# Seven slots for half tiles in each routing in place of eight

## The chip, the cores and the metric

The kernel runs on one core of a Trainium2 chip. The metric is the device time of one execution in microseconds (us). The engines of the core are TensorE (PE, matmuls; PEld is its loading of weights), VectorE (DVE), ScalarE (ACT) and GpSimd (POOL); SyncE (SP) issues most DMA transfers.

## The reference

The kernel computes two layers of a network on 4096 tokens (64 sequences of 64) of width 256, all in float32. The first layer (a scan over the condition, linear attention, a quantised feed-forward net) isn't touched by the change. The second layer has a recurrent net, a selective scan (Mamba), and then two mixtures of experts, one after the other, in each of which every token goes to 2 of 8 experts:

```python
# first mixture: routed experts with one hidden layer of 256, beside two shared experts
s = jax.nn.sigmoid(router_in @ W_router.T)
_, topk_idx = jax.lax.top_k(s + router_bias, 2)
...
for e in range(8):
    h = jax.nn.gelu(x_flat @ r_w1[e].T, approximate=False)
    routed_out = routed_out + h @ r_w2[e].T * gates_full[:, e:e + 1]
out = (shared_out + routed_out) / 4
# second mixture: gated experts with a hidden layer of 704, on the output of the first
topk_scores, topk_idx = jax.lax.top_k(xt @ Wg.T, 2)
y = W3[e] @ (silu(W1[e] @ t) * (W2[e] @ t))       # for the two experts e of token t
out = sum of topk_score * y over the two
```

## The kernel before, in words

**Routing.** A class `Routing` collects, for each expert, the rows of the tokens that chose it. There are three: moe0 and moe1 for the two halves of the tokens in the first mixture (4 chunks of 512 tokens, so 4096 rows for the experts each), and ffn1 for all tokens in the second (8 chunks, 8192 rows). `choose` finds the two experts of each token and the place of its row, `send` scatters the rows (260 numbers: the token's 256, two weights, the token's number and the rank of its first expert) into regions of device memory, one region to an expert, by indirect DMA on POOL (L1357).

**Tiles.** An expert's rows are worked off in whole tiles of 256 rows (`TR`) and half tiles of 128 (`HR`). How many rows an expert gets is known only on the chip; how many tiles run is fixed when the kernel is built. So each routing has slots: `ntl` for whole tiles (16 in moe0 and moe1, 32 in ffn1) and `NHT` for half tiles (8, one for each expert). `Routing.tiles` (L1463) writes a table, made of the counts by a chain of small VectorE instructions, with an expert and a first row for each slot. An expert's remainder of 1 to 128 rows takes a half tile, a remainder above 128 a whole one, and whole tiles for which no slot is left become two halves each. A slot that nobody needs points to filler rows and to expert 0, and is run all the same. The helper `listed` (L1384) fills the table for the whole and for the half slots, `ends` (L1433) makes running sums, `counts` (L1420) gets the counts with one matmul (L1426).

For ffn1, a first table of 8 whole tiles (`EARLY`, L1443) is made when half of the tokens are routed; the remaining 24 whole and all half slots come from `tiles` at the end.

**Running the tiles.** `Experts.run` takes the sections in order; among n whole tiles the halves are spread evenly: after whole tile i come the halves from i * halves // n to (i + 1) * halves // n. For each tile SP reads the expert's number and row from the table (L1637), loads the expert's weights w (L1557; 512 KB in the first mixture, 2176 KB in the second) and the rows gx (L1365), some tiles ahead: 4 in the first mixture (`Gelu`), 2 in the second (`Swiglu`). PE transposes the rows (L1571), VectorE copies them (gxT, L1573) and works out where results go and by what they are weighted (L1576 to L1586). Then:

- `Gelu`: 8 records of up products (L1665), one activation on ACT (rh, L1667), the down products (acc, L1596), weighting on ACT (gy, L1598), scatter on POOL (L1372).
- `Swiglu`: 40 records of up products for the hidden columns in blocks of 128 (L1698) and 4 for the rest (L1706), an activation (gs, L1701) and a product on VectorE (gh, L1702) for each block, then the down products, weighting and scatter as above.

A half tile has the same number of up products with 128 columns in place of 256, half of the transposes and half of the down products. Each logical float32 matmul shows as two records.

**Order of the work.** `mixtures` (L1940) writes the order by hand. Generators are advanced beside the tiles: `tiles_on` steps the tile generator, which yields three times for a tile of the first mixture and nine times in the second, and for each step advances others by a fixed share. Beside moe0's tiles lie the last routing work of moe1 (`rest`) and the last shared experts (L1843, L1859); then the last tiles of moe0 and first of moe1 run alone, while moe1's table is made; beside the rest of moe1 lies the gate of the second mixture for the first four chunks (`gates`: SP loads the shared rows, L1879, and the routed rows, L1381; VectorE adds them, L1886; PE scores them, L1513). The 8 early tiles of ffn1 have the other four chunks beside them, and the last 24 whole and 8 half tiles run alone. The number of tiles in a routing, n + NHT, enters the counts in `tiles_on`. At the end all results are gathered, transposed and added (L2052).

Of the kernel before, what the change touches and what calls it, by code (L numbers as in the profile page):

```python
# [13 lines left out]
F32 = mybir.dt.float32  # L14
# [3 lines left out]
ALU = mybir.AluOpType  # L18
AX = mybir.AxisListType
PSUM = bass.MemoryType.PSUM  # L20

P = 128
# [1129 lines left out]
NE = 8  # L1152
TT = CH // P
TR = 256
HR = TR // 2
NHT = NE
EARLY = 8
assert EARLY * TR <= NT - NE * (TR - 1)

# [90 lines left out]
class Routing:  # L1250
# [10 lines left out]
    def __init__(self, g, pool, x, name, chunks, lots):  # L1261
# [6 lines left out]
        self.taken = None  # L1268
        self.y = g.tc.dram_tile((2 * NT + 2 * TR * (self.ntl + NHT), D), F32, name=f"{name}_y")
        tile = lambda shape, dt, n: pool.tile(shape, dt, name=f"{name}_{n}")  # L1270
# [192 lines left out]
    def tiles(self, pool):  # L1463


        nc = self.g.nc
        ntl = self.ntl - (EARLY if self.taken is not None else 0)
        out = self.tables(pool, ntl + NHT, "tiles")
        with self.g.tc.tile_pool(name=f"{self.name}_table", bufs=1) as work:
            n, first_t = self.counts(work)  # L1470
            col = lambda name: work.tile([P, NE], F32, name=name)

            nk = self.reg // TR
            unit = work.tile([P, NE, 2, nk], F32, name="unit")
            nc.gpsimd.iota(unit, [[0, NE], [HR, 2], [TR, nk]], base=0, channel_multiplier=0, allow_small_or_imprecise_dtypes=True)
            nc.vector.tensor_tensor(unit, n.unsqueeze(2).unsqueeze(3).to_broadcast([P, NE, 2, nk]), unit, ALU.is_gt)
            both = work.tile([P, NE, 2], F32, name="units")
            nc.vector.tensor_reduce(both, unit, AX.X, ALU.add)
            pairs, halves = both[:, :, 1], col("halves")
            nc.vector.tensor_sub(halves, both[:, :, 0], pairs)  # L1480
            if self.taken is not None:
                nc.vector.tensor_sub(pairs, pairs, self.taken)
                nc.vector.scalar_tensor_tensor(first_t, self.taken, float(TR), first_t, ALU.mult, ALU.add)
            begin, end = self.ends(work, pairs, "t")

            over, t = col("over"), col("over_b")
            nc.vector.tensor_scalar(over, end, -float(ntl), 0.0, ALU.add, ALU.max)
            nc.vector.tensor_scalar(t, begin, -float(ntl), 0.0, ALU.add, ALU.max)
            nc.vector.tensor_sub(over, over, t)
            first = col("first_h")  # L1490
            nc.vector.scalar_tensor_tensor(halves, over, 2.0, halves, ALU.mult, ALU.add)
            nc.vector.tensor_sub(first, pairs, over)
            nc.vector.scalar_tensor_tensor(first, first, float(TR), first_t, ALU.mult, ALU.add)
            begin_h, end_h = self.ends(work, halves, "h")
            self.listed(work, out, [(0, ntl, TR, begin, end, first_t), (ntl, NHT, HR, begin_h, end_h, first)])
        return out
# [35 lines left out]
class Experts:  # L1532
# [9 lines left out]
    def run(self, sections):  # L1542
# [71 lines left out]
        def more():  # L1614
            for v in islice(tiles, 1):
                load_rows(v)
                ahead.append(v)
# [322 lines left out]
def mixtures(g, mix, x, weights, out, last, work, close):  # L1940
# [9 lines left out]
    def tiles_on(tiles, n, *beside):  # L1950

        at = 0
        for mark in tiles:
            n -= mark is TILE
            if n == 0:
                break
            at += 1
            for pieces, many in beside:
                some(pieces, int(at * many) - int((at - 1) * many))

    with ExitStack() as ctx:
# [7 lines left out]
        tiles = Gelu(g, (q2, q3, qy, first), weights[0]).run(  # L1969
            [(moe0, lambda: mix.tables, n, NHT, None), (moe1, lambda: tables1[0], n, NHT, None)]  # L1970
        )
        n += NHT
        next(tiles)
        others, shared = mix.rest(last, work, q3), mix.shared(NCH - 1, last, work)
        for _ in range(5):
# [12 lines left out]
        def gates(chunks):  # L1988
# [10 lines left out]
            for c in chunks:  # L1999
# [12 lines left out]
                (routing, lambda: tables2[0], EARLY, 0, routing.sent),  # L2012
                (routing, lambda: tables2[1], ntl, NHT, None),
            ]
# [197 lines left out]
```

## Time and profile before

| | |
|---|---|
| median of 3 runs | 2756.78 us (2755.14 to 2759.66) |
| the profiled execution's own time | 2753.39 us |
| its span, first to last instruction | 2751.5 us |
| mean granted clock of PE | 0.936 |
| moe0 and moe1 tiles | about 1830 to 2133 us |
| early ffn1 tiles | about 2133 to 2265 us |
| last ffn1 tiles | about 2265 to 2707 us |
| gathering and output | to 2751.5 us |
| tables made on VectorE | moe0 up to 1741 us, moe1 1974 to 1980, ffn1 2251 to 2259 |

The profile's summary lists each engine's busy time and its share of the span. The 40 slices are 68.8 us each; a digit is the busy share in tenths, PEclk the clock that PE was granted. A line of the time line has the start in us, the duration, the engine, the source line, the operation, what is written and read, the tile's shape (partitions x elements) and the number of instructions merged; in brackets stands how long the engine was idle before, and who ended that. A line of the waits has the time in total, the number of times and the longest.

### The profile page before, as it was taken

The numbers are of one execution on the slowest core, as the hardware profiler recorded it, in microseconds if no ns is written. First come the engines' busy times: TensorE is split into PE (matmuls) and PEld (weight loads), VectorE is DVE, ScalarE is ACT, GpSimd is POOL, SyncE is SP. The second block draws the span as 40 slices with busy tenths as digits, with TensorE's granted clock in tenths as the row PEclk, the third lists the DMA queues.
The fourth block names the chain that finished last, engine by engine and source line by source line (L and its number), as shares of the span: only waits on it lengthen the run. The fifth ranks groups of instructions, "written<-read, shape, count | busy, mean of one in ns | idle before, by whom it ended". The sixth has DMA issues, their size and how long they took to land.

```text
span 2751.5 us, 34452 instructions
## 1 busy us (share of the span) xinstructions
PE 2310.7 (84%) x11996; PEld 1659.9 (60%) x11996; DVE 1752.4 (64%) x2952; ACT 1398.3 (51%) x2324; POOL 1371.9 (50%) x1194
## 2 busy tenths in 40 slices
PE   3979977997578888887888788788877989999995
PEld 3634435775345555554655555567655778888884
DVE  0467638982899898989889797952353443323333
ACT  0467627884676868685767666643232222222220
POOL 0013345530687878887889797935555331111110
PEclk9989988997769999999999999999998999999997
DMA  9999920002112222221222222226776765555555
GB/s 225 371 358 349 304 72 1 1 1 92 55 62 84 67 77 70 80 70 69 67 96 68 91 70 94 98 77 204 239 263 232 271 231 204 198 197 202 208 195 193
DMA packets 180502, 406.04 MB, mean 148 GB/s; under 512 B 24785, under 2 KB 84434, under 8 KB 174946
## 3 DMA queue, kind: packets, MB, share of 16 engines
q1 hardware_dynamic: 166882, 366.80, 39.0%
q0 software_dynamic: 13440, 36.98, 3.5%
q8 instruction: 96, 1.57, 0.2%
q14 instruction: 84, 0.69, 0.1%
HBM read 280.76 MB, written 144.98 MB: 155 GB/s over the span
## 4 chain that ended last, share of the span: by engine, by line
PE 46%; DVE 22%; ACT 11%; issue 9%; POOL 4%; DMA 2%; another core or an unknown queue 1%; SPq 0%; DVEq 0%; ACTq 0%; POOLq 0%
DVE hb L1108 13%; PE ps L1698 11%; PE acc L1596 9%; PE out L450 4%; DVE hb L1110 3%; PE ps L1665 2%; PE mq L1843 2%; PE yp L1123 2%; ACT dA L1063 2%; PE steps L820 1%; PE s L416 1%; POOL hb L1056 1%; PE acc L441 1%; PE ps L1706 1%; PE mp L919 1%
## 5 line engine op out<-in xcount | busy, mean ns | idle before, releaser
L1056 POOL TENSOR_TENSOR hb<-dx,Bn 128x1024 f32<-128x1024 f32 x256 | 604.9, 2376 | 178.2 <-PE yp L1123 130.8
L1108 DVE TENSOR_TENSOR_SCAN hb<-dA,hb 128x512 f32<-128x512 f32 x512 | 602.3, 1210 | 68.5 <-ACT dA L1063 67.7
L1063 ACT ACTIVATE dA<-delta,negA 128x504 f32<-128x504 f32 x512 | 345.0, 685 | 265.4 <-DVE hb L1108 258.6
L1123 PEld LDWEIGHTS yp<-ident,hb 128*128 128x128 f32 x2048 | 260.1, 149 | 158.4 <-issue 125.2
L1110 DVE TENSOR_TENSOR hb<-hb,cb 128x1024 f32<-128x1024 f32 x256 | 312.4, 1220 | 45.1 <-PE cb L1008 24.7
L1698 PE MATMUL ps<-gxT,w 128*128 128x256 f32 (+1 forms) x1600 | 324.7, 361 | 2.1 <-DVE gh L1702 0.8
L1698 PEld LDWEIGHTS ps<-gxT,w 128*128 128x128 f32 x1600 | 276.2, 190 | 48.4 <-issue 12.4
L1123 PE MATMUL yp<-ident,hb 128*128 128x128 f32 x2048 | 294.6, 286 | 0.0
L1843 PE MATMUL mq<-x,moe_s 128*128 128x256 f32 x896 | 238.2, 399 | 57.8 <-ACT sh L1847 25.8
L1372 POOL DMA_INDIRECT ffn_y<-gy,to x72 | 69.2, 961 | 430.8 <-ACT gy L1598 418.3
L1843 PEld LDWEIGHTS mq<-x,moe_s 128*128 128x128 f32 x896 | 164.3, 196 | 124.1 <-ACT sh L1847 42.9
L1702 DVE TENSOR_TENSOR gh<-gs,ps 128x256 f32<-128x256 f32 (+1 forms) x200 | 78.5, 394 | 211.6 <-ACT gs L1701 199.0
L1598 ACT ACTIVATE gy<-acc,wt 128x256 f32<-128x256 f32 x152 | 67.2, 474 | 250.6 <-PE acc L1596 218.8
L1701 ACT ACTIVATE gs<-ps 128x256 f32<-128x256 f32 (+1 forms) x200 | 72.5, 364 | 237.7 <-PE ps L1698 222.1
L1596 PE MATMUL acc<-w,gh 128*128 128x256 f32 (+1 forms) x864 | 188.2, 388 | 0.0
L1008 PE MATMUL cb<-parts,pick 80*128 80x512 bf16 x256 | 103.3, 404 | 89.2 <-DVE hb L1110 83.3
L1596 PEld LDWEIGHTS acc<-w,gh 128*128 128x128 f32 (+1 forms) x864 | 145.4, 189 | 30.2 <-issue 13.1
L432 POOL TENSOR_TENSOR E<-E,z 128x1024 f32<-128x1024 f32 x32 | 61.6, 1925 | 194.7 <-DVE z L431 117.2
L1372 POOL DMA_INDIRECT moe_y<-gy,to x80 | 77.9, 974 | 98.3 <-ACT gy L1598 73.8
L1596 PE MATMUL acc<-w,rh 128*128 128x256 f32 x320 | 86.3, 411 | 41.4 <-ACT rh L1667 26.4
L450 PE MATMUL out<-oT,hs 128*128 128x512 f32 x256 | 119.4, 611 | 1.5 <-ACT oT L443 1.5
L1859 PE MATMUL mq<-moe_s,sh 128*128 128x256 f32 x448 | 113.3, 386 | 6.6 <-ACT up L1850 2.9
(477 smaller groups left out, 4371.7 us busy)
## 6 DMA issues: line engine op xcount, KB each, us to landing
w<-ffn_w SPq DMA_DIRECT2D x40, 2176.0 KB
Bn<-B SPq DMA_DIRECT2D x128, 512.0 KB
moe_x<-fill SPq DMA_DIRECT2D x130, 260.0 KB
ffn_x<-fill SPq DMA_DIRECT2D x129, 260.0 KB
w<-moe_w SPq DMA_DIRECT2D x48, 512.0 KB
ffn_w<-in_ffn_W_dram SPq DMA_DIRECT2D x16, 640.0 KB
gx<-moe_x SPq DMA_DIRECT2D x32, 260.0 KB
gx<-ffn_x SPq DMA_DIRECT2D x32, 260.0 KB
```

Of the source, the lines that this page charges most:

```text
L450: nc.tensor.matmul(ps, M[:, o, ts(k, P)], v.o[:, o], start=(o == 0), stop=(o == H // 2 - 1))
L1008: nc.tensor.matmul(t, pick[:, n : n + 1].to_broadcast([rows, P]), v.parts, start=True, stop=True)
L1056: nc.gpsimd.tensor_mul(hb, vs[c].dx[p], Bn[:, n % NB, :].unsqueeze(1).to_broadcast([P, PI, CH]))
L1063: nc.scalar.activation(decays[s][i][:, :, 1:], seq(vs[c].delta[p][:, i, :])[:, :, 1:], AF.Exp, scale=A[:, p * PI + i, n : n + 1],)
L1108: ins = nc.vector.tensor_tensor_scan(h, dA[i].rearrange("p b l -> p (b l)"), h, 0.0, ALU.mult, ALU.add)
L1110: ins = nc.vector.tensor_tensor(hb, hb, cb.unsqueeze(1).to_broadcast([P, PI, CH]), ALU.mult)
L1123: nc.tensor.matmul(yp[i][:, t, :], hb[:, i, ts(t, P)], g.ident, start=(n == 0 and t == 0), stop=(n == S - 1 and t == CH // P - 1), is_tran ...
L1372: i = self.g.nc.gpsimd.indirect_dma_start(out=self.y, out_offset=bass.IndirectOffsetOnAxis(ap=to, axis=0), in_=y, in_offset=None)
L1596: nc.tensor.matmul(po[s], h, w, start=(i == 0), stop=(i == n - 1))
L1698: nc.tensor.matmul(ps[:, j, :], v.w12[:, k, ts(j * (full + 1) + i, P)], v.xT[:, k, :], start=(k == 0), stop=(k == KD - 1))
L1843: nc.tensor.matmul(ps[:, i % 2, :], w[:, k, ts(i, P)], xu[:, k, :], start=(k == 0), stop=(k == KD - 1))
L1859: nc.tensor.matmul(ps[:, t, :], h[:, i, ts(t, P)], self.s2[:, i, :], start=(i == 0), stop=(i == NS - 1))
```

## The change

The number of half slots becomes seven. The case in which all eight experts have a remainder of 1 to 128 rows is caught in the table: the minimum of the eight half counts (1 then, else 0) is added to the first expert's whole tiles and taken from its half tiles. The lines of the changed kernel behind the edit are four higher.

```diff
-NHT = NE
+NHT = NE - 1
...
             pairs, halves = both[:, :, 1], col("halves")
             nc.vector.tensor_sub(halves, both[:, :, 0], pairs)
+            all_half = work.tile([P, 1], F32, name="all_half")
+            nc.vector.tensor_reduce(all_half, halves, AX.X, ALU.min)
+            for n_e, sign in ((pairs, 1.0), (halves, -1.0)):
+                nc.vector.scalar_tensor_tensor(n_e[:, 0:1], all_half, sign, n_e[:, 0:1], ALU.mult, ALU.add)
             if self.taken is not None:
```

`NHT` stands in the number of half slots of all three routings, in the size of the table and of the results' buffer, and, through n, in the counts of `tiles_on` for moe0 and moe1. The halves are spread anew among the whole tiles: in ffn1 they stood after every third whole tile (3, 6, ... 24) and stand now after 4, 7, 11, 14, 18, 21 and 24; in moe0 and moe1 after every second one, and now after 3, 5, 7, 10, 12, 14 and 16.

## The prediction

> **What bounds the kernel now.** I read the summary first, then the 40 slices, then PE's time line in the stages that run expert tiles, because a slot is a tile that is run whether its rows are real or filler.
>
> ```profile
> PE 2310.7 (84%) x11996; PEld 1659.9 (60%) x11996; DVE 1752.4 (64%) x2952; ACT 1398.3 (51%) x2324; POOL 1371.9 (50%) x1194
> ...
> PE   3979977997578888887888788788877989999995
> ...
> PEclk9989988997769999999999999999998999999997
> DMA  9999920002112222221222222226776765555555
> ```
>
> No engine is full over the span, but from slice 33 on (2265 us) PE is at 9 tenths at full clock with DMA at 5: that is the last gated layer, with 24 whole and 8 half tiles. The table of stretches says it exactly: PE works in all of 435 us.
>
> ```profile
> 2265.00:2700.00 435.00, 435.00 (x2216) 370.73 (x2215) 132.09 (x473) 94.43 (x251) 54.86 (x58) 1.00 0.54 196
> ```
>
> The first number after the stretch is its length, the second PE's busy time. PE's time line shows one whole tile and the half tile behind it:
>
> ```profile
> 2310.67 8.90 PE L1698 MATMUL ps<-gxT,w 128*128 128x256 f32 x40
> 2319.40 1.03 PE L1706 MATMUL ps<-gxT,w 128*128 128x256 f32 x4
> 2320.27 0.38 PE L1571 MATMUL ps<-ident,gx 128*128 128x128 f32 x2
> 2320.49 5.12 PE L1596 MATMUL acc<-w,gh 128*128 128x256 f32 x24
> 2325.53 4.73 PE L1698 MATMUL ps<-gxT,w 128*128 128x128 f32 x40
> 2330.10 0.61 PE L1706 MATMUL ps<-gxT,w 128*128 128x128 f32 x4
> 2330.55 0.60 PE L1571 MATMUL ps<-ident,gx 128*128 128x128 f32 x4
> 2330.98 2.95 PE L1596 MATMUL acc<-w,gh 128*128 128x256 f32 x12
> 2333.86 2.43 PE L1698 MATMUL ps<-gxT,w 128*128 128x256 f32 x10
> ```
>
> No gap stands before any of them, so here a tile costs what its matmuls cost. The two mixtures (1830 to 2133 us) are another regime: a tile is short, and PE waits in each for ScalarE's activation (rh).
>
> ```profile
> 1987.32 1.99 PE L1596 MATMUL acc<-w,rh 128*128 128x256 f32 x8 [0.53 <-ACT rh L1667]
> 1989.14 1.05 PE L1665 MATMUL ps<-gxT,w 128*128 128x128 f32 x8
> 1990.04 0.60 PE L1571 MATMUL ps<-ident,gx 128*128 128x128 f32 x4
> 1990.73 1.13 PE L1596 MATMUL acc<-w,rh 128*128 128x256 f32 x4
> ...
> 1994.34 1.99 PE L1596 MATMUL acc<-w,rh 128*128 128x256 f32 x8 [0.31 <-ACT rh L1667]
> ...
> 1998.81 1.99 PE L1596 MATMUL acc<-w,rh 128*128 128x256 f32 x8 [0.53 <-ACT rh L1667]
> ```
>
> **What the change removes.** Three half tiles: one in each mixture's routing, one in the last layer. How many tiles run is fixed when the kernel is built, not by the data. The compiled order of instructions says the same: in moe0 and moe1 seven halves stand among 16 whole tiles, in the last layer seven among 24, and the last tile is a half as before.
>
> *Last layer.* From the first half (2325.53) to the next (2378.89 in the same view) is one group of three whole tiles and a half, 53.36 us; the chain of waits has all seven such distances equal. A whole tile between whole tiles takes 15.08 us (2280.50 to 2295.58). The group without its half would take 3 x 15.08 = 45.24, so the half is worth **8.12 us** (8.33 of its own, less 0.22 for the two transposes that its predecessor spares). Every half runs the same instructions, so which slot goes doesn't matter. Its weights (2176 KB) and rows go too; DMA stands at 0.54 of its time there, and PE waits for none of it. I take 8.12 with no play.
>
> By the Trainium skill ("TensorE: Matmul & The Clock Gate", Back-to-back issue gap) a stream of pairs of weight load and matmul sustains about 81 ns each at 128 columns. The row shows (2330.10 - 2325.53) / 40 = 114 ns; by the page the 44 matmuls of 128 columns would take 3.6 us in place of 5.0, and the gain would be an estimated 6.7 us. The row decides.
>
> *The mixtures.* In the uncrowded part, the group of two whole tiles and a half takes 1998.81 - 1987.32 = 11.49 us, and one whole tile behind another 1998.81 - 1994.34 = 4.47. So a half is worth 11.49 - 2 x 4.47 = **2.55 us**. Its PE work alone is near that: from 1989.14 to 1990.04 for the up product, 0.97 for the down product, 0.2 for two transposes, 2.1 in all. Most of the half tiles lie beside other work (the shared experts in moe0, the gate of the last layer in moe1). That work is dealt out by steps of the tile generator, three to a tile, so it stays beside the same number of tiles; with fewer halves among them one more whole tile lies beside it, and the uncrowded end loses one whole tile for it. If that other work, or the transfers, set the pace there, the whole tile is taken in free and the end loses up to 4.47; if what sets the pace cares for neither, nothing is gained. So 0 to 4.47 each, and I take 2.55, the only spacing that the trace shows: 5.10 for two.
>
> **What it adds.** Three small VectorE instructions in each of the three tables: a minimum over eight numbers and two updates of one number. No row has them; the nearest are the neighbours in the same table, here before the last layer:
>
> ```profile
> 2252.28 0.17 DVE L1480 TENSOR_TENSOR halves<-units 128x8 f32<-128x8 f32 x1
> 2252.47 0.17 DVE L1482 TENSOR_TENSOR units<-units,ffn_taken 128x8 f32<-128x8 f32 x1
> 2252.68 0.17 DVE L1439 TENSOR_TENSOR_SCAN endt<-onet,units 128x8 f32<-128x8 f32 x1
> ```
>
> Dependent ones start 0.2 us apart, independent ones 0.08. The minimum and the first update depend on what stands ahead, the second update doesn't: 2 x 0.2 + 0.08 = 0.48; the half-tile lists become 56 wide in place of 64, some 0.08 us less over eleven instructions. So **0.4 us** a table. Nothing hides it in two places. In the last layer's table VectorE works without a pause from 2251.2 to 2259.4, and the products gh (L1702) are queued behind it: PE loses 0.46 + 0.83 + 2.78 us to it today, and each further instruction is added. In moe1's table the copy gxT (L1573) is queued behind, and PE waits 1.56 us for it; SP waits 7.5 us for the table, which four tiles loaded ahead cover. moe0's table lies in the scan stage, where the scans (L1108) are queued behind it. So 0 to 0.6 a table, 0.4 taken, 1.2 in all.
>
> **Moved.** In the compiled order SP's loads of routed and shared rows (L1381, L1879) stand one tile load earlier or later among the loads of w and gx; the number of these row loads is the same, and POOL's scatters become one fewer per half. I cost this at nothing on average; its risk is the last rival.
>
> **Sum.** -8.12 - 5.10 + 1.2 = **-12.0 us**. The profiled execution took 2753.39 (span 2751.5 and 1.9 around it), so it would take 2741.4. It lies 3.4 us below the median of the three runs, 2756.78; against that the change gives **2744.8**. With the bounds: -8.12 - 8.94 + 0 = -17.1 (2739.7), and -8.12 - 0 + 1.8 = -6.3 (2750.5).
>
> **Rivals.** *The mixtures give nothing*: a chain of loads and scatters sets their pace. For it: between 2060 and 2108 us PE is busy only 29.8 of 48 us. Against it: from 1951 to 2013 it is busy 55 of 62, and the spacing of halves there is that of PE and rh. Then only the last layer is gained: -8.12 + 1.2 = -6.9, 2749.9.
>
> *A stall more or less.* Five times ScalarE's rh stands with no releaser that the profile knows:
>
> ```profile
> ACT rh L1667 <- remote: 30.0, 5, 9.2
> ```
>
> That is 30.0 us in all and 9.2 at the longest, at 1942 us, where PE, ScalarE and VectorE all stand while DMA is at 9 tenths and POOL scatters. Afterwards PE runs at half clock: eight products L1665 take 3.4 us where 1.73 is usual, and the four before them 1.9 for 0.9. So a stall costs 6.0 + 2.7 = 8.7 us on average, 11.9 at the longest. By the Trainium skill ("SBUF — State Buffer", Who interferes with whom) DMA never contends with a compute engine, by which moved loads could start no such stall and this rival would be worth 0; the trace shows the coincidence, but no cause. One stall fewer gives 2744.8 - 8.7 = 2736.1. One more gives 2753.5, no change.
>
> *Slower*: two more such stalls in moe1's stretch (2013 to 2108 us), where the row loads that are moved among w and gx meet POOL's scatters; 17.4 to 23.8 us against 12.0, some 2765. It decides from the second extra stall on. Against it: two loads of 512 KB and their rows leave this stretch and the one before.
>
> *It doesn't do what it says*: a slot that stays in the order. The compiled order excludes it: L1665 falls by 16 records, L1698 by 40.
>
> **How the numbers follow.** What a measurement tells from no change is 0.2%, 5.5 us. The sum within its bounds 0.66, the mixtures give nothing 0.10, one stall fewer 0.10, one more 0.08, two more 0.06. The first three are faster: 0.86; same 0.08; slower 0.06. The range goes from 2735 (one stall fewer) to 2752 (above the worst bound, 2750.5); what is left out is 0.14.
>
> **What would show it.** L1698 with 1560 records, L1665 with 368, loads w<-ffn_w 39 and w<-moe_w 46 times. Seven halves in the last layer, each still 8.33 us; from the ffn table to the last matmul 8.1 us less. The stretch 1830 to 2133 shorter by about 5. Tables longer by 0.4, and PE's waits on gh in the last table (4.07 us) longer by as much. I am wrong if the last layer's whole tiles change their 15.08 us, if the mixtures' stretch doesn't shrink, or if the sum of waits without a known releaser moves by more than 9 us.

## The result, and the profile after

The changed kernel takes **2774.3 us** (median of 10 runs, 2767.0 to 2777.9), the kernel before 2759.4 (10 runs, 2754.2 to 2765.5): a ratio of 1.0046, with a 95% interval of 1.003 to 1.0063. It is **slower by 0.5%**, where 12 us less were predicted. The profiled execution took 2772.33 us (span 2770.6), against 2753.39 before.

The last layer did what was forecast. This is PE's time line of the changed kernel there:

```profile
2338.52 8.90 PE L1702 MATMUL ps<-gxT,w 128*128 128x256 f32 x40
2353.60 8.90 PE L1702 MATMUL ps<-gxT,w 128*128 128x256 f32 x40
...
2368.47 4.73 PE L1702 MATMUL ps<-gxT,w 128*128 128x128 f32 x40
...
2376.80 3.50 PE L1702 MATMUL ps<-gxT,w 128*128 128x256 f32 x15
```

A whole tile still takes 2353.60 - 2338.52 = 15.08 us and a half 2376.80 - 2368.47 = 8.33. From the start of the last section's first up product to the start of its last one 414.90 us pass, 423.01 before: **-8.11**, where 8.12 was predicted. The added instructions take 0.16, 0.16 and 0.15 us like their neighbours. PE's three waits at the last table are 5.23 us in sum (4.07 before); of the growth 0.85 lies in the first, ahead of the added instructions, and 0.31 in the two behind them.

Two other stretches lost more than that. The first stands before any tile has run, where moe0's table is made. VectorE's and POOL's time line, before:

```profile
1740.69 0.18 DVE L1411 CAST moe_tiles<-tilesf 128x48 int32<-128x48 f32 x1
1740.79 2.33 DVE L1108 TENSOR_TENSOR_SCAN hb<-dA,hb 128x512 f32<-128x512 f32 x2
1740.81 0.96 POOL L1357 DMA_INDIRECT moe_x<-rows,moe_row  x1 [0.30 <-issue]
1741.80 16.25 POOL L1056 TENSOR_TENSOR hb<-dx,Bn 128x1024 f32<-128x1024 f32 x7
```

and after:

```profile
1737.00 0.96 POOL L1357 DMA_INDIRECT moe_x<-rows,moe_row  x1 [0.30 <-issue]
1737.76 9.52 DVE L1411 CAST moe_tiles<-tilesf 128x46 int32<-128x46 f32 x1
...
1737.99 9.23 POOL L1056 TENSOR_TENSOR hb<-dx,Bn 128x1024 f32<-128x1024 f32 x4
...
1747.20 2.32 DVE L1108 TENSOR_TENSOR_SCAN hb<-dA,hb 128x512 f32<-128x512 f32 x2
```

The last step of the table, a copy that turns 46 numbers a partition into integers (CAST, L1411), takes 9.52 us in place of 0.18: it ends when POOL's four products L1056, which start 0.23 us after it, are done. The scans L1108 are queued behind it. Before, it had come 1.11 us ahead of POOL's run.

The second loss lies in the mixtures: from the first up product of moe0 to the first one of ffn1 298.67 us pass, 285.22 before, though two half tiles less are run. Before, and then after (the stretch, its length, busy time of PE, its weight loads, VectorE, ACT and POOL with counts; the granted clock, the DMA share, GB/s):

```profile
1848.45:2133.67 285.22, 228.81 (x1106) 184.97 (x1106) 109.63 (x546) 86.00 (x175) 149.84 (x170) 0.92 0.69 230
```

```profile
1855.90:2154.57 298.67, 229.08 (x1078) 184.26 (x1078) 105.90 (x533) 84.56 (x171) 149.35 (x168) 0.89 0.64 214
```

PE has two half tiles less to do and is busy just as long, at a lower mean clock (0.89, 0.92 before), and it idles 13 us longer. The waits for which the profile knows no releaser grew for ACT's rh and VectorE's gxT (total, times, longest; before, rh had 30.0, 5 and 9.2, gxT 26.6, 4 and 9.6), while those of ACT's gy fell from 13.8 us to 5.5:

```profile
ACT rh L1671 <- remote: 40.0, 7, 7.8
DVE gxT L1577 <- remote: 50.9, 8, 10.1
```

One of them in the time line of after:

```profile
2118.25 1.05 PE L1669 MATMUL ps<-gxT,w 128*128 128x128 f32 x8
2119.14 0.60 PE L1575 MATMUL ps<-ident,gx 128*128 128x128 f32 x4
...
2125.47 0.96 POOL L1372 DMA_INDIRECT moe_y<-gy,to  x1 [0.30 <-issue]
2127.30 0.38 ACT L1671 ACTIVATE rh<-ps 128x256 f32<-128x256 f32 x1 [7.82 <-remote]
...
2128.70 0.69 DVE L1577 COPY gxT<-ps 128x512 f32<-128x512 f32 x1 [8.26 <-remote]
```

PE's products L1669 are recorded as done at 2119.30 and its transposes L1575 at 2119.74; ACT (rh) and VectorE (gxT), which need them, start 8.0 and 9.0 us later. From 2120.4 to 2127.3 nothing runs but POOL's scatters and transfers. Counted in the time lines, PE, VectorE and ACT all stand for over 2 us five times before (at 1865, 1943, 2042, 2063 and 2095 us; 22.1 us in all) and seven times after (32.7 us).

### The profile page after: what moved, and what is told of

It reads as the page before. It is cut to its first block, busy times and chain, and to the rows that moved or that the text cites. A ratio compares the mean times of both kernels' runs of the same rounds, so it can differ in the third digit from the quotient of the medians.

```text
span 2770.6 us, 34175 instructions
## 1 busy us (share of the span) xinstructions
PE 2310.2 (83%) x11891; PEld 1656.9 (60%) x11910; DVE 1754.3 (63%) x2931; ACT 1392.8 (50%) x2313; POOL 1369.0 (49%) x1191
## 4 chain that ended last, share of the span: by engine, by line
PE 43%; DVE 22%; ACT 11%; issue 9%; POOL 5%; DMA 2%; another core or an unknown queue 2%; SPq 0%; DVEq 0%; ACTq 0%; POOLq 0%
DVE hb L1108 13%; PE ps L1702 11%; PE acc L1600 8%; PE out L450 4%; DVE hb L1110 3%; PE ps L1669 2%; PE yp L1123 2%; PE mq L1847 2%; POOL hb L1056 2%; ACT dA L1063 1%; PE ps L1710 1%; PE acc L441 1%; PE s L416 1%; ACT junk L596 1%
## 5 line engine op out<-in xcount | busy, mean ns | idle before, releaser
L1056 POOL TENSOR_TENSOR hb<-dx,Bn 128x1024 f32<-128x1024 f32 x256 | 605.6, 2378 | 188.5 <-PE yp L1123 139.7
L1108 DVE TENSOR_TENSOR_SCAN hb<-dA,hb 128x512 f32<-128x512 f32 x512 | 602.3, 1210 | 67.7 <-ACT dA L1063 66.8
```

What stands on the lines that cost most here:

```text
L1056: nc.gpsimd.tensor_mul(hb, vs[c].dx[p], Bn[:, n % NB, :].unsqueeze(1).to_broadcast([P, PI, CH]))
L1108: ins = nc.vector.tensor_tensor_scan(h, dA[i].rearrange("p b l -> p (b l)"), h, 0.0, ALU.mult, ALU.add)
```

## The experiments

**Theory A:** the loss begins with the table's copy, which the added instructions push into POOL's run. **Rivals:** the new order of tiles in the mixtures makes it (B, later split into P, the places of the halves, and N, their number), or chance from run to run does (C).

The runs fell on several chips, and these differ. On two of them the kernel before takes some 2712 us, and the waits just shown are absent; on the others it takes 2750 to 2761 and has them, as where the first profiles were made. Each run is compared with the kernel before on its own chip. The table has for each run the difference of the medians, the ratio with its interval, and from its trace the duration of the table's last step in moe0, the length of the mixtures (first L1665 record to first L1698 record), and of the last section. A reduction in place of the cast is written as "red.".

| run | before | differs by | ratio (95%) | last step | mixtures | last section |
|---|---|---|---|---|---|---|
| *chips without the waits* | | | | | | |
| e1: 8 slots, 3 instructions | 2711.7 | +11.6 | 1.0044 (1.0027-1.0062) | 9.88 | 254.1 | 423.0 |
| e12: e1, red. | 2711.8 | -2.0 | 0.9995 (0.9983-1.0008) | 0.20 | 252.1 | 423.0 |
| e2: 7 slots, no instructions | 2711.7 | -14.5 | 0.9946 (0.9929-0.9962) | 0.18 | 254.0 | 414.9 |
| e3: changed kernel, maximum for the cast | 2711.7 | -1.9 | 0.9993 (0.9982-1.0004) | 9.93 | 249.7 | 414.9 |
| e4: ffn1 alone | 2711.7 | -8.9 | 0.9967 (0.9954-0.9979) | 0.18 | 250.9 | 414.9 |
| e9: ffn1 alone, red. | 2711.8 | -10.3 | 0.9965 (0.9954-0.9975) | 0.20 | 252.8 | 414.9 |
| e10: mixtures alone, red. | 2711.8 | -2.9 | 0.9994 (0.9982-1.0006) | 0.19 | 248.2 | 423.0 |
| e11: old places, red. | 2711.8 | -20.0 | 0.9926 (0.9912-0.9940) | 0.20 | 246.6 | 414.9 |
| *chips with the waits* | | | | | | |
| e6: before (profile) | 2750.0 | | | 0.18 | 285.8 | 423.0 |
| e5: changed kernel | 2750.0 | +14.6 | 1.0053 (1.0034-1.0071) | 9.53 | 301.4 | 414.9 |
| e7: changed kernel, red. | 2750.0 | +8.9 | 1.0028 (1.0014-1.0043) | 0.20 | 295.4 | 414.9 |
| e8: 8 slots, 1 instruction | 2750.0 | -0.9 | 0.9992 (0.9976-1.0008) | 0.18 | 279.6 | 423.0 |
| e13: old places, red. (e11) | 2759.2 | -17.0 | 0.9938 (0.9918-0.9958) | 0.20 | 282.4 | 414.9 |
| e14: mixtures alone, red. (e10) | 2759.2 | +14.9 | 1.0049 (1.0032-1.0065) | 0.19 | 305.4 | 423.0 |
| e15: ffn1 alone, red. (e9) | 2759.2 | -8.2 | 0.9966 (0.9950-0.9981) | 0.20 | 285.0 | 414.9 |
| e16: e12 again | 2759.2 | +1.2 | 1.0008 (0.9989-1.0028) | 0.20 | 292.1 | 423.0 |
| e17: 8 slots, halves one tile earlier, red. | 2761.1 | +9.8 | 1.0043 (1.0025-1.0061) | 0.20 | 302.2 | 423.0 |
| e18: 7 slots, odd places, red. | 2761.1 | -3.0 | 0.9998 (0.9976-1.0019) | 0.20 | 300.7 | 414.9 |

### The table's last step

**e1** is the kernel before with the three added instructions, and eight slots (`NHT = NE` in the changed kernel).

> Eight slots as before; only the three added VectorE instructions of each table are kept. Theory A (the cast of moe0's table, L1411 in the changed kernel, is pushed into POOL's run of products L1056 and stands there 9.5 us): the cast takes over 9 us again, the scans behind it are late by as much, and the kernel is about 10 us slower than before, 2766 to 2771 us. Theory B (the loss comes from the new order of whole and half tiles in the mixtures): the cast takes 0.2 us, and the kernel is at most 1.2 us slower than before. Theory C (both are chance from run to run): no difference beyond 2 us, and a cast that is long in one run and short in another.

```profile
1736.32 9.88 DVE L1411 CAST moe_tiles<-tilesf 128x48 int32<-128x48 f32 x1
...
1736.91 9.24 POOL L1056 TENSOR_TENSOR hb<-dx,Bn 128x1024 f32<-128x1024 f32 x4
```

+11.6 us without any slot removed: theory A. The wait goes on to the tiles in full: from the start of this step to moe0's first up product 117.7 to 118.2 us pass in the four runs in which it waits (after, e1, e3, e5), 110.6 in e7 and 107.6 to 108.6 in all others. **e2** takes the slots alone:

```diff
-            all_half = work.tile([P, 1], F32, name="all_half")
-            nc.vector.tensor_reduce(all_half, halves, AX.X, ALU.min)
-            for n_e, sign in ((pairs, 1.0), (halves, -1.0)):
-                nc.vector.scalar_tensor_tensor(n_e[:, 0:1], all_half, sign, n_e[:, 0:1], ALU.mult, ALU.add)
```

> Seven slots, without the three added instructions (the case of eight experts with a half tile each is then not caught). Theory A: the cast takes 0.2 us, and the table's 10 us are back: at most 2764 us, about 10 us less than the changed kernel; if the mixtures' stalls in the changed kernel were also brought by the later start, then all of the predicted gain shows, 2744 to 2748. Theory B: mixtures as long as in the changed kernel (some 299 us from the first moe0 tile to the first ffn1 tile, 285 before), last layer 8 us shorter: before plus 2 to 6 us, 2761 to 2765. In both the cast is short; what tells them apart is the mixtures' stretch.

The cast is short again, and the kernel is 14.5 us faster than before, near what the prediction's sum without its instructions gives (-8.12 - 5.10 = -13.2). That its parts are those of the sum isn't shown: the mixtures of e2's one profile are no shorter than those of eight slots (254.0 against 250.9 to 254.1). **e3** tries another form of the cast in the changed kernel, **e7** a third:

```diff
-        nc.vector.tensor_copy(table, lists)
+        nc.vector.tensor_tensor(table, lists, lists, ALU.max)                  # e3
+        nc.vector.tensor_reduce(table, lists.unsqueeze(3), AX.X, ALU.max)      # e7, "red."
```

> The changed kernel, with the table's cast written as a maximum of the list with itself (TENSOR_TENSOR on VectorE, the same engine, place, size and operands' types in place of CAST). Theory A in its narrow form (it is the form of the cast that has to wait for POOL, not VectorE as a whole): the instruction takes some 0.2 us at the same place, and the kernel takes 9 to 10 us less than the changed one, 2764 to 2766. If any VectorE instruction on float32 would wait there, it stands 9 us again and the time is that of the changed kernel, 2774. Theory B: no more than 2 us of difference from the changed kernel.

> The changed kernel with the table's cast written as a reduction over an axis of one element (TENSOR_REDUCE, one input, no copy); the order of all instructions stays. The maximum of the list with itself stood 9.93 us in the same place as the cast, so it isn't the copy alone that waits. Theory A, with the rule that only one-input forms outside the copy's fast mode pass beside POOL: 0.2 us at that place, and 10 us less than the changed kernel, some 12 us under before where the other waits are absent. Theory A2 (VectorE waits there whatever the form, because something else holds it): 9 to 10 us again, and the changed kernel's time. By the Trainium skill (SBUF — State Buffer, Who interferes with whom) a reduction never contends with GpSimd, and two inputs in SBUF do, as the maximum did.

The step in e3, and then in e7:

```profile
1737.17 9.93 DVE L1411 TENSOR_TENSOR moe_tiles<-tilesf 128x46 int32<-128x46 f32 x1
```

```profile
1738.66 0.20 DVE L1411 TENSOR_REDUCE moe_tiles<-tilesf 128x46 int32<-128x46 f32 x1
```

The narrow form of theory A fell with e3: a maximum of the list with itself waits just as long. With e7 its wider form stands: a reduction with one input passes at the same place in the same order of instructions, in 0.20 us. The whole kernel gained less than the step did: e7's median lies 5.7 us below that of e5, the changed kernel on the same chip, where some 10 were expected; the intervals allow both. The Trainium skill ("SBUF — State Buffer", Who interferes with whom) says that VectorE and GpSimd share one pair of ports, that a copy in its fast mode and an instruction with two inputs in SBUF need it, that a reduction doesn't, and that the loser waits for the whole instruction of the other. The runs agree on who waits; the wait was longer than one instruction, four of POOL's of some 2.3 us each, until POOL had no more to do, and here the measurement decides. By the page the first to issue gets the ports. The copy's record starts ahead of POOL's first product, but POOL's last indirect DMA (1737.00 to 1737.96 in the changed kernel) is under way by then, so the runs don't show in what order the two asked. e3 is the changed kernel in all that matters on a chip without the waits, and shows what is left there: -1.9 us.

The profile before has the effect too, on an instruction with two operands whose like on the second choice (`mine<-score,second`) takes 0.28 us; the prediction didn't look for it:

```profile
1282.05 2.40 POOL L1056 TENSOR_TENSOR hb<-dx,Bn 128x1024 f32<-128x1024 f32 x1 [2.92 <-PE yp L1123]
1282.16 2.43 DVE L1787 TENSOR_TENSOR mine<-score,first 128x128 f32<-128x128 f32 x1
```

**e8** puts one dependent instruction more into each table of the kernel before:

```diff
             nc.vector.tensor_sub(halves, both[:, :, 0], pairs)
+            nc.vector.tensor_scalar(halves, halves, 1.0, None, ALU.mult)
```

> The kernel before with one dependent instruction more in each table (the half counts times 1.0). It puts moe0's cast some 0.2 us later. Three instructions cost 11.6 us. If the loss is a step (the cast either meets POOL's run or doesn't; it went free at 1.11 us ahead of it and was caught at 0.63), this one leaves it at 0.2 us and the kernel is at most 1 us slower than before, or it is already caught, and the kernel is 10 us slower. If each added instruction has its own price, it is a third of 11.6: 3.9 us slower.

```profile
1731.58 0.18 DVE L1411 CAST moe_tiles<-tilesf 128x48 int32<-128x48 f32 x1
...
1732.68 16.25 POOL L1056 TENSOR_TENSOR hb<-dx,Bn 128x1024 f32<-128x1024 f32 x7
```

No loss: a step, not a slope. The cast still stands 1.10 us ahead of POOL's run. The step took 0.18 us where it started 1.10 to 1.26 us ahead (before, e2, e4, e6, e8), and waited where it started 0.23 to 0.63 us ahead (after, e1, e3, e5). The first all start ahead of POOL's last indirect DMA, the second all during it. The reduction took 0.19 to 0.20 us even 0.18 to 0.62 us ahead, during that DMA (e7, e10 to e14, e16, e18).

### Slots, places and the waits in the mixtures

**e5** and **e6** are the two kernels once more.

> The changed kernel itself, once more, beside the others. The run without the cast's changed form gave 1.9 us less than before (2709.8 against 2711.7), although its cast stood just as long, and none of the waits without a known releaser that make 30 us on ACT's rh in the first profile of before. Theory A+S (the cast costs 10 us always; the rest of the loss are those waits, which come on some chips and not on others): without such waits in the profile, before minus 2 us, ratio 0.998 to 1.000; with them, a ratio of 1.003 to 1.006 and 33 us or so of gaps in the mixtures. Theory B (the seven slots themselves make the mixtures longer): ratio 1.004 on any chip.

> The kernel before, for a profile on the same chip. Theory A+S: if the time is near 2712 us, no wait without a releaser and no gap over 2 us in the mixtures, which are 25 to 30 us shorter than the 285 us of the first profile; if near 2757 us, 5 such gaps or so, 20 to 30 us in all. The cast of moe0's table takes 0.2 us in both, 1.1 us ahead of POOL's run of products.

The result repeats (+14.6), on a chip with the waits. **e4** and **e9** have seven slots and the instructions in ffn1 alone (the number becomes an attribute of the routing), e9 with the reduction; **e15** is e9 once more, on a chip with the waits.

> Seven slots and the three instructions in ffn1 alone; moe0 and moe1 keep eight slots and their tables. Theories A and B agree on this one: the moe0 table and the mixtures are those of before, the last layer is 8.1 us shorter, its table 0.4 us longer: before minus 7.7 us, about 2751 us. Theory C (the stalls of the mixtures come and go by chance, from one build to another): anything from 2743 to 2765, with the sum of the gaps in the mixtures in which PE, VectorE and ScalarE all stand between 15 and 35 us (22 before, 33 in the changed kernel).

> Seven slots and the three instructions in ffn1 alone, eight in moe0 and moe1, and the table's cast as a reduction in all three tables. Theory A+S (in the last layer a half slot is worth 8.1 us on every chip; seven slots in the mixtures lose on chips with the unexplained waits): the mixtures are those of before, so before minus 7 to 9 us on either kind of chip, some 2703 where before takes 2712, some 2742 where it takes 2750. Theory B' (any change of the order, as small as in ffn1's table, brings 10 us of waits on a chip that has them): before plus 2 us or more there.

> Seven slots in ffn1 alone, the cast as a reduction, again; 10.3 us faster than before where the waits are absent. If before takes some 2750 us: the mixtures as in before, 280 to 287 us, and 7 to 10 us faster than before; if any small shift brings waits, 290 us or more and no gain.

-8.9, -10.3 and -8.2: the last layer's slot is worth what was predicted, on both kinds of chip. **e10** and **e14** are the other half, the mixtures alone:

> The other half: seven slots and the three instructions in moe0 and moe1, eight in ffn1, the cast as a reduction. Theory A+S: where before takes some 2750 us, the mixtures take 295 to 301 us in place of 285, and the kernel is 12 to 18 us slower than before (8.9 measured with the last layer's gain of 8.1 in it); where before takes some 2712, the mixtures gain 0 to 5 us and cost 0.8 of instructions: minus 5 to plus 1 us. If the loss comes from the three instructions and not from the slots, the mixtures are as long as with eight slots.

> Seven slots in the mixtures alone, the cast as a reduction, again; 2.9 us faster than before where the waits are absent. If before takes some 2750 us: the mixtures take 295 to 301 us and the kernel is 12 to 18 us slower than before, if it is the mixtures' seven slots in their new places that bring the waits; within 5 us of before if it was the last layer's slot or the instructions.

Without the waits -2.9 us, with them **+14.9**, with mixtures of 305 us, a little over the forecast: the loss is there. **e12** and **e16** leave the slots and keep instructions and reduction:

> Eight slots, the three added instructions in each table, the cast as a reduction. It was 11.6 us slower than before with the cast as it is (9.9 of them the cast). Theory A: the cast's 9.3 us are gone, and what is left is the price of the instructions, 0 to 2 us slower than before on either kind of chip. If the instructions also move the phase of the mixtures enough to bring waits, the mixtures are 290 us or longer where before takes some 2750, and the kernel is 5 to 15 us slower there.

> Eight slots, the three instructions, the cast as a reduction, again; 2.0 us faster than before where the waits are absent. If before takes some 2750 us: within 3 us of before and mixtures of 280 to 287 us, if the instructions bring no waits; 5 to 15 us slower and 290 us or more, if they do.

Against e1 (+11.6) e12 is 13.6 us better, more than the 9.7 by which its last step is shorter; the intervals leave that difference open. -2.0 and +1.2: the instructions don't bring the mixtures' loss (e16's one profile has mixtures of 292 us, 7 more than e15's; its median doesn't show them as a loss). **e11** and **e13** keep seven slots, but put the halves where the first seven of eight stood:

```diff
-                    for j in range(i * halves // n, (i + 1) * halves // n):
+                    m = NE if n == 16 else halves
+                    for j in range(min(halves, i * m // n), min(halves, (i + 1) * m // n)):
```

> The changed kernel with the cast as a reduction, and in moe0 and moe1 the seven halves stand where the first seven of eight stood, after every second whole tile up to the fourteenth; the last tile is a whole one then. Theory P (the places of the halves, which set the phase of tiles against loads and scatters, make the waits): the mixtures take 280 to 288 us where before takes some 2750, and the kernel is 8 to 13 us faster than before. Theory N (the number of slots, and with it the shares of the work beside them, does): 295 to 301 us there, and some 9 us slower than before, like the changed kernel with the reduction. Where before takes some 2712 us the two can't be told apart: 7 to 13 us faster than before.

> The kernel with the halves of the mixtures in their old places, again; it gave 20.0 us less than before where the unexplained waits are absent (before 2711.8). If before takes some 2750 us here: theory P (the places make the waits) 280 to 288 us of mixtures and 8 to 20 us faster than before; theory N (the number of slots does) 295 to 301 us and 5 to 12 us slower. If before takes some 2712: 20 us faster again.

-20.0 (more than the 7 to 13 that were forecast) and -17.0 us: **theory P**. The places are what costs: e13 without the last section's -8.1 is at -8.9, against +14.9 of e14 on the same chip. And this version is faster than both kernels on both kinds of chip. The waits without a known releaser in e13 and in e14, on the same chip:

```profile
ACT rh L1672 <- remote: 28.1, 3, 10.6
DVE gxT L1577 <- remote: 24.4, 4, 9.6
```

```profile
ACT rh L1673 <- remote: 44.0, 8, 8.1
DVE gxT L1579 <- remote: 45.8, 8, 10.0
```

52.5 us against 89.8. The two engines mostly wait at the same time, so the sums aren't the loss, and ACT's gy has 14.0 us of such waits more in e13 and none in e14. The stretches of over 2 us in which PE, VectorE and ACT all stand in the mixtures are 27.6 us in 5 against 35.5 in 8. **e17** moves the eight halves of the kernel before one whole tile ahead, **e18** has seven after the third, fifth, ... fifteenth tile:

```diff
+                    for j in range((i + 1) // 2, min(halves, i // 2 + 1)) if n == 16 else ...   # e17
+                    for j in range((i - 1) // 2, i // 2) if n == 16 and i else ...              # e18
```

> The kernel before with the cast as a reduction, and in moe0 and moe1 the eight halves stand after the first, third, ... fifteenth whole tile in place of the second, fourth, ... sixteenth. Work, slots and tables are those of before. Theory P in its wide form (any other places of the halves bring more of the unexplained waits where a chip has them): mixtures of 290 us or more and 5 to 20 us slower than before, if before takes some 2750 us. Theory P in its narrow form (only the changed kernel's places do, with their two pairs of three whole tiles between halves): mixtures of 278 to 288 us and within 5 us of before. Where before takes some 2712 us: within 5 us of before in both.

> The changed kernel with the cast as a reduction, and the seven halves of moe0 and moe1 after the third, fifth, ... fifteenth whole tile. The changed kernel has them after 3, 5, 7, 10, 12, 14 and 16, the fast one after 2, 4, ... 14. If the waits come by the tile's number being odd where the work beside it is dealt out: like the changed kernel, mixtures of 295 us or more and 5 to 12 us slower than before, if before takes some 2750 us. If they come by the late halves of the changed kernel (after 10 to 16): mixtures of 280 to 290 us and 8 to 17 us faster than before. Where before takes some 2712 us: 10 to 20 us faster in both.

e17 loses 9.8 us with no slot removed and mixtures of 302 us: the wide form of P, for the places tried here. e18 has the long mixtures of the first alternative (300.7) but its time (-3.0 by the medians, none by the ratio) lies between the two forecasts; neither of its sizes was right. All three engines stand for 26.3 us there, as long as in e6 (26.4), so these stands alone don't make its mixtures long.

**What the waits are.** The same place of the program, a half tile of moe0 in eight slots, in e6 and then in e4 (whose lines are six higher there):

```profile
1943.41 1.05 PE L1665 MATMUL ps<-gxT,w 128*128 128x128 f32 x8
...
1954.07 0.39 ACT L1667 ACTIVATE rh<-ps 128x256 f32<-128x256 f32 x1 [9.84 <-remote]
```

```profile
1926.69 1.05 PE L1671 MATMUL ps<-gxT,w 128*128 128x128 f32 x8
...
1927.84 0.38 ACT L1673 ACTIVATE rh<-ps 128x256 f32<-128x256 f32 x1 [1.34 <-PE ps L1671]
```

And the table of 2 us stretches behind it (columns as in the table of the mixtures), e6:

```profile
1944.00:1946.00 2.00, 1.76 (x13) 1.31 (x11) 0.82 (x5) 0.22 (x1) 1.83 (x3) 1.00 1.05 395
1946.00:1948.00 2.00, 0.00 (x0) 0.00 (x0) 0.00 (x0) 0.00 (x0) 1.39 (x3) 1.00 1.05 411
...
1950.00:1952.00 2.00, 0.00 (x0) 0.00 (x0) 0.00 (x0) 0.00 (x0) 1.39 (x3) 0.50 0.86 307
...
1954.00:1956.00 2.00, 1.50 (x4) 1.23 (x5) 0.71 (x2) 0.98 (x2) 0.76 (x4) 0.50 0.00 0
```

and e4:

```profile
1928.00:1930.00 2.00, 2.00 (x12) 1.77 (x11) 0.76 (x2) 0.87 (x3) 1.53 (x4) 1.00 1.08 412
...
1932.00:1934.00 2.00, 1.69 (x9) 1.44 (x8) 0.48 (x4) 0.35 (x2) 1.39 (x3) 1.00 1.07 387
1934.00:1936.00 2.00, 1.23 (x6) 0.77 (x5) 1.09 (x5) 0.89 (x2) 1.68 (x4) 1.00 1.09 420
```

In both, the DMA engines are full (1.05 to 1.09, 387 to 420 GB/s in the first rows). In e4 the activation starts 0.1 us behind the products and PE works on; in e6 it starts 9.6 us behind them, about when the transfers have run off, and PE comes back at half clock. So a full DMA stands beside this wait, but isn't enough for it. What ACT and VectorE wait for on those chips, and why the places of the halves decide what that costs, is open; a kernel with less traffic there wasn't tried. Also open is the early ffn1 section, 146.8 us before and 153.8 after: with eight slots in the mixtures it took 147.0 to 152.6 on chips with the waits (e6, e8, e15, e16, e17), so most of its growth doesn't need the slots. ACT's gs has waits of 2.5 and 5.7 us without a known releaser there in the changed kernel and none over 2 us before; e16, with eight slots, has 2.4 and 5.7.

## Why the prediction was wrong

- **Right: the last layer.** -8.11 us in every trace with seven slots there, against -8.12. By the rate of the Trainium skill ("TensorE: Matmul & The Clock Gate", Back-to-back issue gap) it would have been an estimated 6.7; the row was right, not that rate.
- **Wrong: "So 0 to 0.6 a table, 0.4 taken".** The step counted the instructions' own time, and that was right (0.31 us more of PE's waits behind them in the last table). But in saying that "the scans (L1108) are queued behind it" in moe0's table it stopped at the chain's length and didn't look at what POOL ran beside its end. There the copy into the table stood 1.11 us ahead of a run of POOL's products that it can't pass. In its place: 9.3 to 9.8 us in one table (9.52 to 9.93 less 0.18). The profile before had both rows. The sum on a chip without the waits is then -12.0 + 9.5 = -2.5, and e3 measured -1.9; in part that is luck, for by the profiles the mixtures there save 1.8 us, not 5.1.
- **Wrong: the mixtures' "So 0 to 4.47 each, and I take 2.55".** Without the waits seven slots took 248.2 to 254.0 us where eight took 250.9 to 254.1, -1.8 in the mean (3 and 4 profiles), inside these bounds but well under the 5.1 taken. With the waits, seven in the new places took 295.4 to 305.4 (after, e5, e7, e14), where eight in the old ones took 279.6 to 292.1 (before, e6, e8, e15, e16). The bounds were made from what a half tile costs, not from what its place does.
- **Wrong: "Moved. I cost this at nothing on average", with the rival of two more stalls at 0.06.** The rival's mechanism is the one that came, if not in moe1's stretch alone: all three engines stand seven times in place of five, once more in moe0 and once more in moe1, and ACT's waits on rh moved by 10.0 us, past the 9 that the prediction named as a sign of being wrong. The mixtures got 13 to 16 us longer (298.7 - 285.2, 301.4 - 285.8) where 5.1 less was taken, a difference of 19 to 21, inside the rival's 17.4 to 23.8. The fault is the zero and the weight: the step took the stalls of one trace as chance events. They return at the same tiles where the order is the same (at 1866, 1946, 2040, 2083 and 2097 us in e6, four of the five at the tiles of before; after, e5 and e7 have six in common), and grow when the halves are moved by one tile (37.6 us in e17, 26.4 in e6).
- Together: -8.1 of the last section, some +9.5 of the copy, +13.5 of the mixtures and +7 of the early ffn1 section are +21.9, and the spans of the two profiles lie 19.1 us apart; most of the rest is that the stages up to moe0's table ran 3.9 us shorter in that one profile. They vary: the table's last step starts at 1728.3 to 1741.1 us in the profiles of all runs, so that such sums over single profiles close only by some us.

## What to carry to other kernels

Ahead of adding even a few short instructions to a chain on VectorE, look at what GpSimd runs beside the chain's end: an instruction that reads two operands from SBUF, or copies there, may have to wait for all of a run, and the price is a step of that run's length; a one-input reduction passed. Where a trace has waits without a known releaser, another order of work can bring more of them, so take work out and keep the places of the rest: on chips with the waits seven halves in old places gave -17 us (e13), in new ones +9 (e7). And price a slot by the spacing of tiles only where an engine is full, as here in the last layer.

## What was not expected of the hardware

- The step that ends the table waited although its record starts 0.23 to 0.63 us ahead of POOL's first product, and it waited for four products in a row (9.24 us in e1), not for one. In each such run POOL's last indirect DMA was under way when it started.
- Chips differ for one and the same kernel: 2711.7 and 2711.8 us on two, 2750.0 to 2761.1 on the others. Of the 43 us from 2711.7 to the 2754.7 of e6's own execution, some 33 lie in the mixtures (285.8 us in e6, 250.9 to 254.1 with eight slots on the first two).
